# Down with seven products for five of seven pairs of weight tiles in blocks 2 and 3, and sums of GLU tiles made by adding stores to DRAM

## The chip, the core and the metric

The kernel runs on one core of one Trainium2 chip. The metric is device time in microseconds (us); the time of a kernel is the median of its runs. One execution is recorded by the hardware profiler, and its page and its trace are what this text reads. Times inside the execution count from the start of its span.

## What is computed

The input is x of shape 4 x 512 x 512, that is 2048 tokens of 512 features. The result is x plus two branches that both start from the layer-normalised tokens xn: a long convolution (S4), and a gated feed-forward network (GLU) whose three weight matrices are given as 4-bit codes with one scale for 64 values.

```python
xn = layernorm(x)                                # over the last axis
K  = s4_kernel(Lambda, p, q, B, Ct, step, 512)   # 512 taps
y  = causal_conv(xn, K) + D * xn                 # along the last axis
g  = xn @ dequant(gate_q).T                      # M = 1792 hidden features
u  = xn @ dequant(up_q).T
h  = silu(g) * u
out = x + y + h @ dequant(down_q).T
```

All of it has to come out with fp32 accuracy.

## The kernel before

**Accuracy.** TensorE multiplies in fp32r. Each operand that needs it is split into three parts, called high, low and e, and a product is three matmuls. The helper `split` makes the parts: ScalarE copies with a scale (L179), VectorE subtracts (L181), VectorE combines (L183). `split_scaled` and the Down variant at L1206 to L1210 do the same for weights.

**Tiles.** The hidden features are cut into 14 tiles of 128 rows, named m = 0 to 13; two neighbours form a pair p = m // 2, so there are seven pairs. The tokens are cut into four blocks of 512, named tb = 0 to 3. One hidden tile (m, tb) is 128 partitions x 512 numbers, 256 KB.

**Stages.** The head (layer norm, transposes, the convolution's taps, m = 0 and 1) is written out by hand, then come m = 2 to 4 and the convolution (`conv`: matmuls of 512, 384 and 256 columns at L662, of 128 at L667, evictions at L672). In m = 5 to 8 the token blocks 0 and 1 are done by Strassen's seven products in place of eight (`products_pair`), blocks 2 and 3 the standard way; in m = 9 to 13 both pairs of blocks take seven products (`products_both`, L626). Then comes Down, whose products are made block by block.

**Order.** From m = 5 on, steps are put on a list with a due time by `at(time, what, ...)`. The list is sorted, and the instructions of ScalarE, VectorE, TensorE and GpSimd are each chained in that order. SyncE's queue works in the order of the program too. An instruction that waits holds up all that stands behind it on its engine.

**Hidden tiles.** `silu` (L542, ScalarE) writes a tile h, `gated` multiplies it by the up product (L546, VectorE), and `store_hidden` (L549 and L550) stores it to the DRAM tile hd of its block and pair by SyncE, 56 stores of 256 KB. With seven products a tile u is also used: `copy_p5` (L974, ScalarE) keeps the fifth product in it, `add_up0` (L977) and `add_up1` (L981) add it, and `gated1` (L994) turns it into a finished tile, which is stored from there. The tiles live in five slots h0 to h4, which are used again and again: u in slots 0 and 1 by the pair of blocks, h in slots 2, 3 and 4. A slot is free again when its store has landed.

**Down weights.** The Down codes are loaded, turned into weights by a chain of bends (L314 on ScalarE, L324 on VectorE) and a multiplication, and stored to the DRAM tiles wdd, one for each pair, 512 KB (`down_weights` in the stretch of m = 2 to 4, `scale_down` for the last two pairs).

**Down.** For block tb and pair p, `down_product` makes 4 token tiles j x 2 weight tiles k x 3 parts = 24 matmuls of 128 x 512 (L697); 28 such steps are 672 matmuls. `load_hidden` (SyncE) brings the raw tile pair from hd into the tile stage, `hidden_part` splits it into hp; `load_split` (GpSimd, L1197) and `split_down` do the same with the weights during block 0, after which all seven pairs of weight parts stay in wdt. `load_rest` (GpSimd, L704) brings x plus the convolution from the DRAM tile rd into the tile late (1 MB a block), and `finish` (L709, VectorE) adds the bank and sends the result out.

The due times of block 0 and of what follows are set like this (STEP is 24 matmuls, D0 the start of Down):

```python
for i in range(NTB * NPR):
    tb, p = divmod(i, NPR)
    o = STEP * i
    when.setdefault(i, (
        [o + t for t in ((-8.1, -5.6, -4.45) if tb == 0 else (-11.0, -9.2, -7.8))],
        [o + t for t in (-9.2, -8.0, -6.8)],
    ))
```

Of the kernel before, what the change touches and what calls it, by code (L numbers as in the profile page):

```python
# [16 lines left out]
P = 128  # L17
# [80 lines left out]
def layernorm_s4_nf4_glu_kernel(  # L98
# [63 lines left out]
    h_dram = [[tc.dram_tile([P, 2, 512], F32, name=f"hd{b}_{p}") for p in range(NPR)] for b in range(NTB)]  # L162
    wd_dram = [tc.dram_tile([P, 2, 512], F32, name=f"wdd{p}") for p in range(NPR)]
# [21 lines left out]

    def split_scaled(dst, src):
        S.activation(dst[0], src, AF.Copy, scale=TRIM / LAM)
        V.scalar_tensor_tensor(dst[1], f(dst[0]), -LAM, src, ALU.mult, ALU.add)
        V.scalar_tensor_tensor(dst[2], src, 1.0 / OUT, f(dst[0]), ALU.mult, ALU.subtract)
# [125 lines left out]

    def parts_tile(n):
        return place([P, 3, 2, 512], F32R, f"wp_{n}")

    def decode(pair):
        if pair not in qs:  # L320
            load_weights(pair)
        q, sc, n = qs.pop(pair)
        bends(q, range(len(BENDS)))
        V.tensor_tensor(q, q, sc, ALU.mult)  # L324
        return q, n
# [219 lines left out]
    def gated(m, tb, pu, h, unit):  # L545
        V.scalar_tensor_tensor(h, pu, unit, h, ALU.mult, ALU.mult)  # L546
        store_hidden(m, tb, h)

    def store_hidden(m, tb, h):  # L549
        nc.sync.dma_start(h_dram[tb][m // 2][:, m % 2, :], h)  # L550
# [13 lines left out]
    def sums_of_tokens():  # L564
# [24 lines left out]
        whole_of(t2, x12)  # L589
        V.tensor_tensor(t2, t2, t0, ALU.subtract)  # L590
        split_scaled(s4, t2)
# [90 lines left out]

    def load_hidden(tb, p):
        nc.sync.dma_start(stage[0][:, 2 * ((tb * NPR + p) % 3), :, :], h_dram[tb][p])

    def hidden_part(tb, p, k):
        if k == 0:
            hp[tb, p] = place([P, 3, 2, 512], F32R, f"hp{tb}_{p}", (tb * NPR + p) % 4)
        split([hp[tb, p][:, i, :, :] for i in range(3)], stage[0][:, 2 * ((tb * NPR + p) % 3), :, :], (k,))

    def banks_down(tb):
        return [K[i] for i in ((6, 7, 0, 3), (1, 2, 4, 5))[tb % 2]]

    def down_product(tb, p, j):
        for k in range(2):
            for part in range(3):
                T.matmul(  # L697
                    banks_down(tb)[j], hp[tb, p][:, part, k, bass.ts(j, P)], wd(p, part, k),
                    start=(p == 0 and k == 0 and part == 0),
                    stop=(p == NPR - 1 and k == 1 and part == 2),  # L700
                )

    def load_rest(tb):
        nc.gpsimd.dma_start(late["x"][:, 0:4, :], res_dram[tb])  # L704

    def finish(tb, j):
        for i, cs in enumerate(HALVES if j == 3 and tb == NTB - 1 else (ALL,)):
            o = late["x"][:, j, cs]
# [6 lines left out]
    def down_weights(p):  # L715
        nc.sync.dma_start(wd_dram[p], decode(dd(p))[0])
# [419 lines left out]
    at(begin(5) + 1.4, open_area, "turn", 3)  # L1136
# [18 lines left out]
    def load_down_scales(p, k=None):  # L1155
# [3 lines left out]
        late["x"] = phase[0].tile([P, 6, 512], F32, tag="xs4", name="late", bufs=1)  # L1159
        q, _, n = qs[dd(p)]  # L1160
        qs[dd(p)] = (q, late["x"][:, 4:6, :], n)
# [30 lines left out]

    def open_down():
        stage.append(phase[0].tile([P, 6, 2, 512], F32, tag="xs12", name="stage", bufs=1))

    def load_split(p):
        nc.gpsimd.dma_start(stage[0][:, 2 * (p % 3) + 1, :, :], wd_dram[p])  # L1197

    def split_down(p, k):
        for i in range(len(wdt), (6 * p + 9) // 4):  # L1200
            wdt.append(work.tile([P, 4, 512], F32R, tag="xp", name=f"wdt{i}", bufs=12))
        at = [6 * p + 2 * i for i in range(3)]
        d = [wdt[s // 4][:, s % 4 : s % 4 + 2, :] for s in at]
        src = stage[0][:, 2 * (p % 3) + 1, :, :]
        if k == 0:
            S.activation(d[0], src, AF.Copy, scale=TRIM / LAM)  # L1206
        elif k == 1:
            V.scalar_tensor_tensor(d[1], f(d[0]), -LAM, src, ALU.mult, ALU.add)
        else:
            V.scalar_tensor_tensor(d[2], src, 1.0 / OUT, f(d[0]), ALU.mult, ALU.subtract)  # L1210
# [9 lines left out]
    for i in range(NTB * NPR):  # L1220
        tb, p = divmod(i, NPR)
        o = STEP * i
        when.setdefault(i, (
            [o + t for t in ((-8.1, -5.6, -4.45) if tb == 0 else (-11.0, -9.2, -7.8))],
            [o + t for t in (-9.2, -8.0, -6.8)],
        ))
        for k in range(3):
            at(D0 + when[i][0][k], hidden_part, tb, p, k)
            if tb == 0:
                at(D0 + when[i][1][k], split_down, p, k)  # L1230
        at(D0 + (-12.19 + 0.04 * i if i < 3 else when[i - 3][0][2] + 0.1), load_hidden, tb, p)
        if tb == 0:
            at(D0 + (-12.19 + 0.04 * p if p < 3 else max(when[p - 3][1][2] + 0.1, 12.1 if p == 6 else 0.0)), load_split, p)
        for j in range(4):
            at(D0 + o + 6 * MM * j, down_product, tb, p, j)
            if p == NPR - 1:
                at(D0 + o + 6 * MM * (j + 1) + 0.3, finish, tb, j)
    for tb in range(1, NTB):
        at(D0 + STEP * NPR * tb + 8.0, load_rest, tb)
# [91 lines left out]
```

## Time and profile before

| | us |
|---|---|
| median of 3 runs | 495.94 (495.21 to 496.44) |
| profiled execution, own time | 495.62 |
| its span | 493.7 |
| m = 9 begins (first product, TensorE) | 242.1 |
| m = 10 begins | 261.2 |
| Down begins | 337.2 |
| last matmul ends | 490.0 |
| TensorE busy | 488.4 |
| VectorE busy | 361.7 |
| ScalarE busy | 298.2 |
| GpSimd busy | 18.6 |

| DMA issues | engine | count | KB each | median us from issue to landing |
|---|---|---|---|---|
| hd<-h | SyncE | 42 | 256 | 2.0 |
| hd<-u | SyncE | 14 | 256 | 2.0 |
| stage<-hd | SyncE | 28 | 512 | 4.3 |
| stage<-wdd | GpSimd | 7 | 512 | 7.2 |
| late<-rd | GpSimd | 4 | 1024 | 9.2 |

Over the span the DMA engines move 81.65 MB, 165 GB/s on the mean. The clock granted to TensorE is full in all 40 slices of the page.

How to read the lines: PE is TensorE's matmuls, PEld its weight loads (which overlap), DVE is VectorE, ACT ScalarE, POOL GpSimd, SP SyncE. A group line gives line, engine, operation, out<-in, how often, then busy time and mean ns of one, then the idle time of the engine ahead of the group and what ended it. A timeline line gives start, length, engine, line, operation, and in brackets the idle time ahead. A matmul's length is longer than the distance to the next one's start, as matmuls overlap.

### The profile page before, as it was taken

Reading aid. Unit: us, or ns where it says so; the run is one execution under the profiler, and the core shown is the slowest. Engines: PE = TensorE matmul, PEld = TensorE weight load, DVE = VectorE, ACT = ScalarE, POOL = GpSimd, SP = SyncE. Lnnn points to the kernel's source line nnn. Section 1 sums busy time; section 2 is a strip of 40 time slices with the busy share of each in tenths; the row PEclk is TensorE's granted clock in tenths of the full one; section 3 lists DMA queues with packets and bytes.
Section 4 is the critical chain, followed back from the end, with each engine's and each line's share of the span. In section 5 each row is a group of like instructions: output and inputs, shape, how many; then the busy total and the mean of one; then the engine's idle time right before and its main releaser. Section 6 shows DMA issues by size and latency. Waiting matters only on the chain.

```text
span 493.7 us, 6400 instructions
## 1 busy us (share of the span) xinstructions
PE 488.4 (99%) x2257; PEld 409.4 (83%) x2257; DVE 361.7 (73%) x576; ACT 298.2 (60%) x417; POOL 18.6 (4%) x35
## 2 busy tenths in 40 slices
PE   8999999999999999999999999999999999999996
PEld 8888888888988888888888888888888888888885
DVE  5999788969459779988896776859989527437412
ACT  7998869994856787684858967849632111211200
POOL 2302000000000000000000000010000000000000
PEclk9999999999999999999999999999999999999999
DMA  8943274957895133233223323369847525624302
GB/s 291 324 147 122 63 227 152 283 182 273 271 308 171 39 112 108 73 119 129 86 86 141 114 86 136 112 237 375 308 135 260 206 86 175 209 85 162 137 0 85
DMA packets 35983, 81.65 MB, mean 165 GB/s; under 512 B 4592, under 2 KB 5104, under 8 KB 34928
## 3 DMA queue, kind: packets, MB, share of 16 engines
q1 hardware_dynamic: 34080, 73.00, 43.2%
q0 software_dynamic: 1584, 7.87, 4.5%
q10 hardware_dynamic: 288, 0.39, 0.2%
q8 instruction: 17, 0.28, 0.2%
q14 instruction: 14, 0.11, 0.1%
HBM read 54.50 MB, written 26.74 MB: 165 GB/s over the span
## 4 chain that ended last, share of the span: by engine, by line
PE 99%; POOL 0%; issue 0%; DVE 0%; DVEq 0%; POOLq 0%
PE bank L697 31%; PE bank L626 27%; PE gu L522 17%; PE bank L635 9%; PE pc L662 5%; PE bank L522 3%; PE gu L530 3%; PE warm L744 2%; PE pt L240 1%; PE pc L667 1%; PE pm L494 0%; PE pss L405 0%; PE pm L489 0%; DVE late L709 0%; DVEq L1327 0%
## 5 line engine op out<-in xcount | busy, mean ns | idle before, releaser
L697 PE MATMUL bank<-wdt,hp 128*128 128x512 f32 x672 | 152.8, 389 | 0.0
L697 PEld LDWEIGHTS bank<-wdt,hp 128*128 128x128 f32 x672 | 126.0, 188 | 26.7 <-DVE hp L183 0.4
L179 ACT ACTIVATE hp<-stage 128x1024 fp32r<-128x1024 f32 x28 | 29.4, 1056 | 81.7 <-PE bank L697 65.4
L181 DVE TENSOR_TENSOR hp<-stage,hp 128x1024 fp32r<-128x1024 f32 x28 | 34.2, 1221 | 29.3 <-ACT hp L179 29.2
L709 DVE SCALAR_TENSOR_TENSOR late<-bank,late 128x512 f32<-128x512 f32 (+1 forms) x17 | 10.8, 657 | 33.3 <-PE bank L697 33.3
L542 ACT ACTIVATE h<-bank 128x512 f32<-128x512 f32 x39 | 22.9, 591 | 20.1 <-PE bank L626 15.4
L183 DVE SCALAR_TENSOR_TENSOR hp<-hp 128x1024 fp32r<-128x1024 f32 x28 | 34.3, 1224 | 0.9
L522 PE MATMUL gu<-xhT,wp_gu 128*128 128x512 f32 x112 | 29.8, 394 | 0.0
L522 PE MATMUL gu<-xlT,wp_gu 128*128 128x512 f32 x112 | 29.1, 389 | 0.0
L522 PE MATMUL gu<-xeT,wp_gu 128*128 128x512 f32 x112 | 28.8, 389 | 0.0
L626 PE MATMUL bank<-xlT,turn 128*128 128x512 f32 x82 | 25.3, 389 | 0.0
L626 PE MATMUL bank<-xeT,turn 128*128 128x512 f32 x82 | 25.3, 389 | 0.0
L626 PE MATMUL bank<-xhT,turn 128*128 128x512 f32 x82 | 25.2, 389 | 0.0
L522 PEld LDWEIGHTS gu<-xlT,wp_gu 128*128 128x128 f32 x112 | 21.0, 188 | 4.4
L522 PEld LDWEIGHTS gu<-xeT,wp_gu 128*128 128x128 f32 x112 | 21.0, 188 | 4.4
L522 PEld LDWEIGHTS gu<-xhT,wp_gu 128*128 128x128 f32 x112 | 20.8, 188 | 4.2
L626 PE MATMUL bank<-xs,turn 128*128 128x512 f32 x90 | 22.8, 389 | 0.0
L626 PEld LDWEIGHTS bank<-xs,turn 128*128 128x128 f32 x90 | 16.9, 188 | 3.5
L546 DVE SCALAR_TENSOR_TENSOR h<-bank,h 128x512 f32<-128x512 f32 x25 | 16.8, 685 | 2.3 <-PE bank L626 1.3
L626 PE MATMUL bank<-xs_s,turn 128*128 128x512 f32 x72 | 18.3, 389 | 0.0
L626 PEld LDWEIGHTS bank<-xeT,turn 128*128 128x128 f32 x82 | 15.4, 188 | 3.2
L626 PEld LDWEIGHTS bank<-xlT,turn 128*128 128x128 f32 x82 | 15.4, 188 | 3.2
(338 smaller groups left out, 973.0 us busy)
## 6 DMA issues: line engine op xcount, KB each, us to landing
stage<-hd SPq DMA_DIRECT2D x28, 512.0 KB, 4.3
hd<-h SPq DMA_DIRECT2D x42, 256.0 KB, 2.0
xr<-in_x_dram SPq DMA_DIRECT2D x4, 1024.0 KB, 7.0
rd<-xr SPq DMA_DIRECT2D x4, 1024.0 KB, 4.9
late<-rd POOLq DMA_DIRECT2D x4, 1024.0 KB, 9.2
out_dram<-late SPq DMA_DIRECT2D x15, 256.0 KB, 2.8
hd<-u SPq DMA_DIRECT2D x14, 256.0 KB, 2.0
stage<-wdd POOLq DMA_DIRECT2D x7, 512.0 KB, 7.2
```

The source lines that it names most:

```text
L179: S.activation(dst[0], src, AF.Copy, scale=TRIM)
L181: V.tensor_tensor(dst[1], src, f(dst[0]), ALU.subtract)
L183: V.scalar_tensor_tensor(dst[2], f(dst[1]), -LAM, f(dst[0]), ALU.mult, ALU.add)
L522: T.matmul(ps, wp[:, part, k, bass.ts(c, P)], xT[tb][part][:, :, c, :], start=(part == 0 and c == 0), stop=(part == 2 and c == NC - 1),)
L530: T.matmul(ps[:, k, j.start * P : j.stop * P], w[:, k, bass.ts(c, P)], xf[tb].rearrange("p j (c q) -> p j c q", c=NC)[:, j, c, :], start=( ...
L542: S.activation(h, pg, AF.Silu, scale=unit)
L546: V.scalar_tensor_tensor(h, pu, unit, h, ALU.mult, ALU.mult)
L626: T.matmul(ps, w[:, part, bass.ts(c, P)], x[part][:, :, bass.ts(c, P)], start=(first and part == 0 and c == 0), stop=(part == 2 and c == 1 ...
L635: T.matmul(ps, blocks[c // 2][:, part, bass.ts(c % 2, P)], xT[tb][part][:, :, c, :], start=(part == 0 and c == 0), stop=(part == 2 and c = ...
L662: T.matmul(po[:, k, i * P : HD], xT[tb][part][:, jj + k, i, :], toep[:, part, 0 : HD - i * P], start=(i == 0 and part == 0), stop=False,)
L697: T.matmul(banks_down(tb)[j], hp[tb, p][:, part, k, bass.ts(j, P)], wd(p, part, k), start=(p == 0 and k == 0 and part == 0), stop=(p == NP ...
L709: V.scalar_tensor_tensor(o, banks_down(tb)[j][:, cs], OUT, o, ALU.mult, ALU.add)
```

## The change

1. **Seven products in Down.** For blocks 2 and 3 and pairs 0 to 4, the eight quarter products (two blocks, two weight tiles k, two halves of 256 output columns) become seven, p1, p5, p6, p2, p7, p3 and p4 in this order over the five pairs each, with matmuls of 256 columns (`down_blocks`). Pairs 5 and 6 of these blocks stay as they were and lie between: (2,5) behind p2, (3,5) behind p7, (2,6) behind p3, (3,6) at the end. Blocks 0 and 1 are as before. Sums of products are formed in the banks: `copy_first` and `keep_fifth` (ScalarE, 8 copies) and `add_fifth` (VectorE, 8 additions).
2. **Sums of hidden tiles.** Four of the seven products need sums of hidden tiles. They are made in new DRAM tiles sd (one for each of the five pairs, four rows of 256 KB): `store_hidden` sends each tile of blocks 2 and 3 there by GpSimd's queue, into a range of rows, the first writer of a row plainly, the later ones with `accum_op=add`. These are 23 transfers: 15 that add (one of 1 MB, eight of 768 KB, one of 512 KB, five of 256 KB) and 8 plain ones. For the signs, the tiles of block 2 of these pairs are negated in `gated`. Five stores to hd are dropped (block 3, k = 0).
3. **Sums of weights.** Four sums of quarter tiles for each pair: for pairs 0 to 2 in `down_weights`, in the tile of the scales, stored to new DRAM tiles td; for pairs 3 and 4 in Down, from the weights loaded again (`prepare_sums`). `sums_part` splits them, during block 1, into places that have come free.
4. **Places.** The tile stage is cut otherwise; the rows of `load_rest` become four tiles in the slots h0 to h3 with four loads of 256 KB a block; the places of hp change. In the stretch of m = 5, the last of the token sums (s4) and its split move from ahead of m = 5 into it, and the area "turn" is opened 6.0 us into m = 5 and not 1.4.

The core of the diff:

```diff
     def gated(m, tb, pu, h, unit):
-        V.scalar_tensor_tensor(h, pu, unit, h, ALU.mult, ALU.mult)
+        V.scalar_tensor_tensor(h, pu, unit_of(m, tb, unit), h, ALU.mult, ALU.mult)
         store_hidden(m, tb, h)
+    def unit_of(m, tb, unit):
+        return -unit if m // 2 < NSP and tb == 2 else unit
     def store_hidden(m, tb, h):
-        nc.sync.dma_start(h_dram[tb][m // 2][:, m % 2, :], h)
+        p, k = divmod(m, 2)
+        if (tb, k) != (3, 0) or p >= NSP:
+            nc.sync.dma_start(h_dram[tb][p][:, k, :], h)
+        if p < NSP and tb >= 2:
+            lo, hi = {(2, 0): (0, 3), (3, 0): (0, 4), (2, 1): (2, 3), (3, 1): (1, 4)}[tb, k]
+            new = [i for i in range(lo, hi) if (p, i) not in summed]
+            for a, b, op in (
+                (lo, hi - len(new), ALU.add), (hi - len(new), hi, ALU.bypass),
+            ):
+                if a < b:
+                    nc.gpsimd.dma_start(
+                        s_dram[p][:, a:b, :], h.unsqueeze(1).to_broadcast([P, b - a, 512]),
+                        accum_op=op,
+                    )
+            summed.update((p, i) for i in new)
...
     def down_weights(p):
-        nc.sync.dma_start(wd_dram[p], decode(dd(p))[0])
+        q, _ = decode(dd(p))
+        nc.sync.dma_start(wd_dram[p], q)
+        if p < EARLY:
+            t = scales_of[dd(p)]
+            sums_of_weights(quarters(t), q)
+            nc.sync.dma_start(t_dram[p], t)
+    def sums_of_weights(t, q):
+        (t1, t3, t4, t2), (b11, b12, b21, b22) = t, quarters(q)
+        V.tensor_tensor(t1, b11, b12, ALU.subtract)
+        V.tensor_tensor(t3, b22, b12, ALU.subtract)
+        V.scalar_tensor_tensor(t2, t1, -1.0, b22, ALU.mult, ALU.subtract)
+        V.scalar_tensor_tensor(t4, t2, -1.0, b21, ALU.mult, ALU.subtract)
...
+    def down_blocks(pair, j):
+        for n, p in pair:
+            tb, half = {"p2": (2, left), "p3": (2, right), "p5": (3, right)}.get(n, (3, left))
+            for part in range(3):
+                T.matmul(
+                    banks_down(tb)[j][:, half], blocks_in[n, p][part][:, bass.ts(j, P)],
+                    block_weights(n, p, part),
+                    start=(n == "p1" and p == 0 and part == 0), stop=False, skip_group_check=True,
+                )
+    def copy_first(j):
+        S.copy(banks_down(2)[j][:, left], banks_down(3)[j][:, left])
+    def keep_fifth(j):
+        S.copy(kept_of(j), banks_down(3)[j][:, right])
+    def add_fifth(tb, j):
+        V.tensor_tensor(
+            banks_down(tb)[j][:, right], banks_down(3)[j][:, left], kept_of(j), ALU.add
+        )
...
+    SUMS_AT = (-4.5, 2.0, 8.0, 14.5, 25.0)
+    t = D1
+    for p in range(NPR):
+        if p < NSP:
+            units.append((D1 + SUMS_AT[p], None, load_sums, (p,), sums_part, (p,), None))
+        t = standard(1, p, t, 3 if p == 0 else next_place())
+    for n, what in (("p1", (copy_first,)), ("p5", (keep_fifth,)), ("p6", (add_fifth, 2)), ("p2", ())):
+        t = seven(n, t)
+        if what:
+            after(t, *what)
+    t = standard(2, 5, t, next_place())
+    t = seven("p7", t)
+    after(t, add_fifth, 3)
+    t = standard(3, 5, t, next_place())
+    t = seven("p3", t)
+    t = standard(2, 6, t, next_place())
+    t = seven("p4", t)
+    at(t - 4.0, load_rest, 3)
+    t = standard(3, 6, t, next_place())
...
-    at(begin(5) + 1.4, open_area, "turn", 3)
+    at(begin(5) + 6.0, open_area, "turn", 3)
```

`seven(n, t)` puts the 12 matmuls of each of the five pairs on the list and registers the loads of the blocks (`load_blocks`, SyncE, 35 transfers of 256 KB from hd and sd) and their splits; `standard` does so for a step of 24 matmuls. A loop behind them gives each load and split a due time: in the order in which TensorE needs them, on VectorE 1.25 us for each part, into three rotating places.

## The prediction

> **What bounds the kernel now.** I read the page's busy shares first, then the chain that ended last, then the costliest groups.
>
> ```profile
> PE 488.4 (99%) x2257; PEld 409.4 (83%) x2257; DVE 361.7 (73%) x576; ACT 298.2 (60%) x417; POOL 18.6 (4%) x35
> PE 99%; POOL 0%; issue 0%; DVE 0%; DVEq 0%; POOLq 0%
> L697 PE MATMUL bank<-wdt,hp 128*128 128x512 f32 x672 | 152.8, 389 | 0.0
> ```
>
> TensorE works without a gap: the chain is 99% PE, and the 672 Down matmuls of L697 have no idle time before them and take 152.8 us, 227 ns each from start to start (the 389 ns are one instruction's length; they overlap). So every matmul saved counts in full, and every wait that is put before TensorE counts in full too. The table by stretches, cut at the four Down blocks, shows what room the other engines have there (columns: stretch, us, then busy time and instructions of PE, PEld, DVE, ACT, POOL, granted clock, DMA share, GB/s):
>
> ```profile
> 337.20:375.30 38.10, 38.10 (x168) 31.13 (x167) 36.11 (x35) 21.80 (x24) 2.63 (x5) 1.00 0.73 260
> 375.30:413.40 38.10, 38.10 (x170) 31.55 (x169) 20.28 (x20) 7.43 (x7) 0.53 (x1) 1.00 0.46 157
> 413.40:451.50 38.10, 38.10 (x169) 31.55 (x169) 19.31 (x19) 7.43 (x7) 0.53 (x1) 1.00 0.46 153
> 451.50:490.00 38.50, 38.50 (x170) 31.54 (x169) 15.30 (x15) 4.25 (x4) 0.53 (x1) 1.00 0.28 97
> ```
>
> VectorE is full in block 0 (36.1 of 38.1 us) and half idle in blocks 1 to 3; DMA has room from block 1 on.
>
> **TensorE's own sum.** Five of seven pairs of blocks 2 and 3 were 5 x 2 x 24 = 240 matmuls of 512 columns and become 7 x 5 x 4 x 3 = 420 of 256 columns. 512 columns cost 227 ns. For 256 columns in fp32r with a fresh weight tile each, the trace has only the convolution's runs of three:
>
> ```profile
> 127.16 0.28 PE L662 MATMUL pc<-tp,xhT 128*128 128x256 f32 x1
> 127.27 0.28 PE L662 MATMUL pc<-tp,xlT 128*128 128x256 f32 x1
> 127.39 0.28 PE L662 MATMUL pc<-tp,xeT 128*128 128x256 f32 x1
> ```
>
> Starts lie 0.11 and 0.12 us apart; over all 32 such gaps the median is 117 ns, the range 116 to 127. So -240 x 0.227 = -54.4 and +420 x 0.117 = +49.1: **-5.3 us**; at 127 ns it is -1.1.
>
> The Trainium skill, "TensorE: Matmul & The Clock Gate" (Wait — 56ns, not 53.3ns?), gives the gap of a warm clock as columns / 2.4 GHz + about 2.5 ns: 215.8 ns for 512 and 109 for 256, which would make it -51.8 + 45.8 = -6.0 and the whole sum -3.2. The rows (227 and 117) are both longer, so they decide.
>
> **VectorE in block 1.** The weight sums of all five pairs need parts, and the change puts them into the start of block 1. From 367.93, where the low part of the last block-0 tile starts before and after, VectorE has ahead of hp1_2: 9 operations of 1024 elements up to the low part of hp1_1, with 3 evictions (L709) between; rows of this stretch start 1.13 us apart (1.26 where one needs the other), and an eviction takes 0.60:
>
> ```profile
> 366.80 1.22 DVE L1210 SCALAR_TENSOR_TENSOR wdt<-stage,wdt 128x1024 fp32r<-128x1024 f32 x1
> 367.93 1.22 DVE L181 TENSOR_TENSOR hp<-stage,hp 128x1024 fp32r<-128x1024 f32 x1
> 369.19 1.23 DVE L183 SCALAR_TENSOR_TENSOR hp<-hp 128x1024 fp32r<-128x1024 f32 x1
> ```
>  So 367.93 + 9 x 1.13 + 3 x 0.60 + 0.1 = 380.0. This frees the place for the raw weights of pair 3, which land after about 0.3 + 4.3 (the median of stage<-hd, 512 KB) = 384.5; the operations left before are done by 384.1. Then four sums of 256 elements (1.5), hp1_2's low part (1.26) and its third part (1.2) end at 388.5. TensorE comes to the third part at 375.3 + 2 x 5.45 + 0.45 = 386.65. Wait: **+1.8 us**; 0 if VectorE gets ahead by an idle gap, 3 if that load takes the longer landings of this stretch. In blocks 2 and 3 the added work (8 copies of ScalarE, 8 additions and the splits of VectorE) falls on half idle engines, and of the copied banks only those added to after p7 are needed at once, by the standard products of pair 5. I cost it at 0; without that cover the addition after p7 costs 0.3.
>
> **The adding stores.** They go through GpSimd's queue, 23 transfers (9.2 MB adding, 5.2 MB plain), each behind the landing of the earlier store to the same sd tile. A hidden tile's slot is held until they land. The nearest place is at the start of m=10, where the ring of slots turns fastest:
>
> ```profile
> 262.63 1.75 SPq L550 DMA_DIRECT2D hd<-u  x2
> 266.76 1.06 ACT L974 COPY u<-bank 128x512 f32<-128x512 f32 x2
> 268.51 0.69 DVE L977 TENSOR_TENSOR bank<-bank,u 128x512 f32<-128x512 f32 x1
> ```
>
> The second store of L550 (u9_1) is issued at 264.06 and lands at 266.06; the second copy of L974 writes that slot at 267.24. Behind the copy wait a ring part on ScalarE, its low part on VectorE, and then the addition L977, which ends 1.96 us after the copy starts; p7 needs it at 272.06. So the copy can start as late as 270.1: a 768 KB adding store may take 6.0 us from issue to landing, and from then on TensorE waits one for one. No adding transfer is in the trace. Bounds: GpSimd's one transfer with the queue to itself,
>
> ```profile
> DMA to landing us min/median/max: 3.5/3.5/3.5
> ```
>
> (512 KB; first packet 1.2 us after issue, 2.0 us of packets, 0.3 to landing) makes 1.2 + 3.0 + 0.3 = 4.5 us for 768 KB. If the destination is read as well as written, so that packets take twice as long, 7.5. The queue's rows in a busy stretch (512 KB in 7 to 10 us, 1 MB in 6.2 to 11.0) reach 11. GpSimd's own 0.53 us for a transfer, in rows whose packets are some 5 KB (1584 packets for 7.87 MB on the page), may grow by about 1 with the 2 KB rows here, which lies inside these bounds. I take 7, near the doubled one, since this stretch has little other traffic: **+1.0 us**, between 0 and 5. Elsewhere in m=5 to m=9 the slots are reused some 15 us after their store, which covers up to about 10 us a transfer; GpSimd does nothing else there.
>
> The Trainium skill, "DMA: Bandwidth & Descriptors" (Anatomy of one DMA; Rules for kernel authors), gives 2.0 us + bytes / 436e3 for a transfer of this queue, an estimate of 3.8 us, no wait and a sum of -3.5; the same page says that an accumulating DMA must wait for the semaphore of an earlier one on the same bytes, which speaks against the change, as it makes chains of these stores. No run here shows the rate of one that adds.
>
> **What goes at nothing.** The down codes q_d6d come later: SyncE's queue now has the stores of the sums of pairs 1 and 2 (waiting for VectorE) and one rd store ahead of them, about 8 us. Its consumers end their evictions at 146.06 and TensorE asks for that bank at 155.06, so 9.0 us of cover; up to +1 if it is used up. The 12 operations of weight sums (0.33 us each) before m=5 and the token sums moved into m=5 lie beside TensorE's work on engines that are 60 to 73% busy. SyncE's five fewer hidden loads of 512 KB, 35 of 256 KB and five reloads in Down meet a DMA share of 0.46 and less. The five hd stores dropped save no time on the path.
>
> **Sum.** -5.3 + 1.8 + 1.0 = **-2.5 us**. The profiled execution took 495.62 us (span 493.7 and 1.9 around it), 0.3 below the median of 495.94; from it 493.1, from the median **493.4 us**.
>
> **The rivals.** (a) *The adding stores run near the plain rate* (4.5 to 6 us): no wait at m=10; for it speaks the small share of DMA in m=9, against it the second read. -5.3 + 1.8 = -3.5, 492.4; if VectorE also keeps up, 490.6. (b) *Slower: the adding stores are slow.* One mechanism, at the slot of u9_1: its store must also wait for the 256 KB add of h9_2, issued at 260.25. With 1.5 us fixed and b us per 256 KB, it lands at 260.25 + 3.0 + 4b once b is over 2.3. At the contended rows' 11 us (b = 3.2) that is 276.1, a wait of 6.0: -5.3 + 1.8 + 6.0 = +2.5, 498.4. At b = 4.2 (14 us) it is 280.1, 10.0 of wait, 502.4, and from there stores pile up in m=6 to m=9 as well. It decides, by over 0.3%, from b of about 3.0 or 10.6 us per 768 KB. For it: reading and writing DRAM for each of 2 KB rows, on a queue whose contended rows are slow. Against it: DMA has half its time free in that stage. (c) *256 columns do not hold 117 ns over hundreds.* LDWEIGHTS is 188 ns long and only overlaps, and runs of three prove little. At 127 ns, -1.1 + 2.8 = +1.7; with the waits partly hidden, about 495 to 497.5, no change. (d) *The change does not do what it says*, TensorE's count as before: excluded by the loops, which leave 432 + 420 Down matmuls.
>
> **How the numbers follow.** A measurement of this kernel can tell about 0.3%, 1.5 us, from no change: faster is below 494.45, slower above 497.43. The forecast (short waits, 492.4 to 494.4) 0.40; (a) 0.18; (c), or a wait that eats the gain, 0.14; (b) 0.28. Faster 0.58, same 0.14, slower 0.28. The range runs from 490.2 (no wait, shorter gaps) to 502.0 (b up to 14 us a store), which leaves out slower stores still, about 0.15, and little below. The likeliest sign's own range is 490.2 to 494.4.
>
> **What would show it.** Right: 420 matmuls of 256 columns 117 ns apart; TensorE idle about 1.8 us ahead of hp1_2 and about 1 at m=10's p7; a 768 KB adding store landing in 6 to 8 us. Wrong: landings over 10 us with L974 waiting for a DMA; a gap of 127 or more; any idle time of TensorE over 1 us elsewhere, above all in m=5 or at the bank of the convolution.

## The result, and the profile after

The changed kernel takes **520.33 us**, the median of 4 runs (518.85 to 522.06), against 495.57 for the kernel before beside it: 1.050 times the time, with a 95% interval of 1.046 to 1.054. The prediction was 493.4, with a range up to 502.0: 2.5 us faster was forecast, and it is 24.8 us slower. The profiled execution took 522.06 us with a span of 520.4. Of all the runs told here, two of the sums from DRAM to DRAM (532.1 and 534.5 us) fell into a slower state of the machine and are left out of its ratio.

The page of the changed kernel: engines, granted clock, GpSimd's DMA queue (packets, MB, share of 16 engines), the chain by engine (it can be followed back to 274.95 us, so its shares add up to less than 100%), and the costliest group.

```profile
PE 495.7 (95%) x2437; PEld 419.4 (81%) x2437; DVE 401.1 (77%) x641; ACT 314.1 (60%) x443; POOL 48.5 (9%) x70
PEclk9999999989998999999999899999999889999999
q0 software_dynamic: 8416, 22.29, 19.2%
PE 28%; DMA 8%; DVE 6%; issue 3%; ACT 1%; DVEq 0%; ACTq 0%; POOLq 0%
L750 PE MATMUL bank<-wdt,hp 128*128 128x512 f32 x336 | 80.9, 401 | 6.1 <-DVE hp L185 3.6
```

TensorE has the 180 matmuls more that the change asks for, but the chain, 99% PE before, is now mixed with DMA and VectorE, and the clock dips in four places. The Down group had 0.0 us of idle time ahead of it and has 6.1. So TensorE waits. Where it does is read from the same landmarks in both traces (start times after minus before), each stretch with what held TensorE at its largest gap:

| stretch | predicted, us | measured, us | what TensorE waited for |
|---|---|---|---|
| up to the convolution's first matmul | 0 | +4.6 | VectorE, behind ScalarE, behind a late load of codes of m = 5 (9.1 us to land, 4.5 before) |
| convolution, m = 2 to 4 | 0 | +5.3 | a bank of the convolution, emptied late, since the down codes were loaded late |
| m = 5 to 8 | 0 | +1.9 | small waits, the first part of the one at 265 |
| m = 9 to 13 | +1.0 | +8.3 | copies that wait for a slot: 2.2 at 265 (for a plain store of u that took 5.3 us beside an adding one, 2.0 before), 5.9 at 290 |
| Down | -5.3 + 1.8 | +6.7 | -4.1 of matmuls, +10.8 of waits (2.0 at 390, 7.8 at 408, 1.1 at 453) |
| sum | -2.5 | +26.8 | |

**The predicted place.** GpSimd's and ScalarE's timeline around the slot of u9_1, then the chain that ended last:

```profile
274.95 0.90 POOL L580 DMA_DIRECT2D sd<-h  x1 [19.92 <-DVE h L560]
280.14 1.27 POOL L580 DMA_DIRECT2D sd<-u  x1 [4.29 <-DVE turn L187]
288.21 0.58 ACT L1049 COPY u<-bank 128x512 f32<-128x512 f32 x1 [6.44 <-DMA sd<-u]
```
```profile
280.14 7.91 DMA sd<-u
290.23 54.89 PE bank L662 x234
```

The 256 KB add of h9_2 is issued at 274.95 and lands 4.7 us later; only then may the 768 KB add of u9_1 start, at 280.14, though u9_1 was ready at 278.5. This one takes 7.91 us, the copy (L1049, the old L974) waits 6.44 us for it, and TensorE starts again at 290.23, after 4.1 us of idle time and 4.3 us later than its usual step. The gap is not the whole price. The table by windows of the trace (us, busy time and instructions of PE, PEld, DVE, ACT, POOL, granted clock, DMA share, GB/s):

```profile
285.70:290.20 4.50, 0.42 (x2) 0.00 (x0) 1.06 (x3) 1.99 (x5) 0.00 (x0) 0.99 0.38 98
290.20:293.70 3.50, 3.47 (x9) 2.74 (x10) 3.43 (x9) 1.02 (x3) 0.00 (x0) 0.53 0.61 181
293.70:297.00 3.30, 3.30 (x16) 2.72 (x15) 3.16 (x7) 3.24 (x5) 0.00 (x0) 1.00 0.15 47
```

After the gap the clock is 0.53 for 3.5 us: 9 matmuls instead of 16. So this wait cost 4.3 + 1.6 = 5.9 us. The gaps that end at 106 (2.9 us idle), 163 (3.3) and 412 (3.6) are followed by a slow clock too, the last one for twice as long; the gap of 1.7 us that ends at 392 is not. The wait at 265 is shorter:

```profile
262.54 0.59 ACT L1049 COPY u<-bank 128x512 f32<-128x512 f32 x1 [4.36 <-DMA hd<-u]
```

Here the same copy waits for a plain store of u, to hd, which landed after 5.3 us. In the kernel before that store landed 0.5 us ahead of the copy.

**Ahead of the convolution.** The first line is TensorE's gap, the second ScalarE's wait ahead of it, the third the two stores to sd (768 KB adding, 256 KB plain) that run at that time and take 10.3 and 10.6 us to land:

```profile
106.20 0.80 PE L503 MATMUL pm<-s4b,s4b 128*128 128x128 f32 x2 [2.85 <-DVE s4b L498]
102.47 2.15 ACT L325 ACTIVATE q_g5u<-q_g5u 128x1024 f32<-128x1024 int32 x2 [6.27 <-DMA sc_g5u<-in_up_s_dram]
91.18 1.93 POOL L580 DMA_DIRECT2D sd<-h  x2 [0.71 <-DVE nqi L458]
```

ScalarE starts when the up codes q_g5u have landed, at 102.45 (9.1 us after their issue, 4.5 before; the load of scales that the line names lands later, at 102.83). Behind it in the order of the engines come a silu, a VectorE product and the step of the taps that TensorE waits for. No slot is in this chain: the stores to sd cost time here by slowing a load beside them.

**The convolution.** The first line is VectorE waiting for a slot of a hidden tile, in which the tokens xn of the convolution are to be put; the second is SyncE's issue of the first load of the down codes q_d6d, which was at 119.17 before; the third says why (time waited, times, longest):

```profile
132.78 0.69 DVE L685 SCALAR_TENSOR_TENSOR xn<-xhT,xlT 128x512 f32<-128x512 f32 x1 [4.65 <-DMA sd<-h]
133.70 0.33 SPq L299 DMA_DIRECT2D q_d6d<-in_down_q_dram  x1
```
```profile
SPq L299 <- DMA wdd<-q_d2d: 5.2, 1, 5.2
```

The store wdd<-q_d2d has nothing to do with the sums. It took 9.0 us to land where it had taken 2.6, beside an adding store. So the first load of the down codes came 14.5 us later, and the second, which ScalarE needs to begin, 16.7, as a store of rd ahead of it had to wait for VectorE. ScalarE's start, in the kernel before and in the changed one, and TensorE's gap:

```profile
125.22 8.71 ACT L314 ACTIVATE q_d6d<-q_d6d 128x1024 f32<-128x1024 int32 x8 [3.50 <-issue]
142.13 8.71 ACT L325 ACTIVATE q_d6d<-q_d6d 128x1024 f32<-128x1024 int32 x8 [4.01 <-issue]
163.03 1.48 PE L536 MATMUL bank<-xhT,wp_g4u 128*128 128x512 f32 x4 [3.33 <-DVE xr L708]
```

ScalarE is 16.9 us later and TensorE itself 4.6, so the codes lost 12.3 us against it. The prediction's cover of 9.0 leaves 3.3, which is the gap.

**Down.** In the chain, one transfer stands before the largest gap; VectorE then waits at the head of the sums for pair 3:

```profile
401.07 8.48 DMA stage<-wdd
```
```profile
409.57 0.43 DVE L788 TENSOR_TENSOR kept<-stage 128x256 f32<-128x256 f32 x1 [4.45 <-DMA stage<-wdd]
```

The prediction had this load land after 4.6 us; it took 8.48, and hp1_2 is split behind it. No adding store runs then: what lands beside it are three loads of load_rest of block 1 (6.4 to 8.6 us each) and output stores.

**The matmuls.** TensorE's rows of p-products in Down: 3 matmuls each, 0.36 us apart.

```profile
459.11 0.52 PE L1397 MATMUL bank<-wdt,stage 128*128 128x256 f32 x3
459.47 0.52 PE L1397 MATMUL bank<-tw,stage 128*128 128x256 f32 x3
```

The median over 416 such gaps is 120 ns, so TensorE's own sum is -240 x 0.227 + 420 x 0.120 = -4.1 us, not -5.3.

### The profile page after: what moved, and what is told of

It reads as the page before. It is cut to its first block, busy times and chain, and to the rows that moved or that the text cites. A ratio compares the mean times of both kernels' runs of the same rounds, so it can differ in the third digit from the quotient of the medians.

```text
span 520.4 us, 7020 instructions
## 1 busy us (share of the span) xinstructions
PE 495.7 (95%) x2437; PEld 419.4 (81%) x2437; DVE 401.1 (77%) x641; ACT 314.1 (60%) x443; POOL 48.5 (9%) x70
## 3 DMA queue, kind: packets, MB, share of 16 engines
q0 software_dynamic: 8416, 22.29, 19.2%
## 5 line engine op out<-in xcount | busy, mean ns | idle before, releaser
L750 PE MATMUL bank<-wdt,hp 128*128 128x512 f32 x336 | 80.9, 401 | 6.1 <-DVE hp L185 3.6
L750 PEld LDWEIGHTS bank<-wdt,hp 128*128 128x128 f32 x336 | 64.7, 194 | 21.1 <-DVE hp L185 4.0
L580 POOL DMA_DIRECT2D sd<-h x22 | 21.7, 1052 | 205.3 <-DVE h L560 176.9
L1378 ACT ACTIVATE hb_p<-stage 128x1024 fp32r<-128x1024 f32 (+1 forms) x14 | 12.3, 877 | 30.9 <-PE bank L750 20.0
L662 PEld LDWEIGHTS bank<-xhT,turn 128*128 128x128 f32 x82 | 15.4, 194 | 11.2 <-DVE bank L1052 7.1
L183 ACT ACTIVATE hp<-stage 128x1024 fp32r<-128x1024 f32 x14 | 14.7, 1052 | 13.2 <-PE bank L750 4.4
L750 PE MATMUL bank<-wdt,stage 128*128 128x512 f32 x96 | 22.5, 390 | 0.0
L185 DVE TENSOR_TENSOR hp<-stage,hp 128x1024 fp32r<-128x1024 f32 x14 | 17.1, 1221 | 5.5 <-ACT hp L183 5.5
L750 PEld LDWEIGHTS bank<-wdt,stage 128*128 128x128 f32 x96 | 17.9, 188 | 3.6
L1380 DVE SCALAR_TENSOR_TENSOR hb_p<-stage,hb_p 128x1024 fp32r<-128x1024 f32 (+1 forms) x14 | 13.9, 992 | 8.4 <-ACT hb_p L1378 8.4
```

What stands on the lines that cost most here:

```text
L183: S.activation(dst[0], src, AF.Copy, scale=TRIM)
L185: V.tensor_tensor(dst[1], src, f(dst[0]), ALU.subtract)
L580: nc.gpsimd.dma_start(s_dram[p][:, a:b, :], h.unsqueeze(1).to_broadcast([P, b - a, 512]), accum_op=op,)
L662: T.matmul(ps, w[:, part, bass.ts(c, P)], x[part][:, :, bass.ts(c, P)], start=(first and part == 0 and c == 0), stop=(part == 2 and c == 1 ...
L750: T.matmul(banks_down(tb)[j], hp[tb, p][part][:, k, bass.ts(j, P)], wd(p, part, k), start=(first and k == 0 and part == 0), stop=(last and ...
L1378: S.activation(d[0], src, AF.Copy, scale=-TRIM)
```

## The experiments

The main theory: the adding stores cost the time, by what they make wait and by slowing each transfer beside them. Its rivals: the sums of weights made early (VectorE, stores to td in SyncE's queue) cost it; or Down's own order does, and the seven products save nothing. The kernels are told in groups by what they tell apart.

### Which part costs: stores, additions, weight sums

**No stores to sd**; the products of Down read other hidden tiles (the sums are left out), the rest is as in the changed kernel.

```diff
-        if p < NSP and tb >= 2:
+        if False:
...
-            return s_dram[p][:, SOURCE[n], :]
...
+            return h_dram[tb][p][:, k, :]
```

> The changed kernel without the 23 stores to sd; the Down steps load other tiles of the same size from hd in their place (so the sums are left out). TensorE's idle gaps in the changed kernel, with the slow clock behind them: 3.5 us at 106, 5.2 at 163, 2.2 at 265, 5.9 at 290, then in Down 2.0 at 392, 7.8 at 412 and 1.1 at 453. Theory 1 (the stores to sd hold hidden slots and crowd the other transfers): the four gaps ahead of Down go, 520 - 16.8 = about 503. Theory 2 (the sums of weights, their stores and the order of SyncE's queue make the gaps at 106 and 163; sd only those at 265 and 290): about 512.

Measured: 499.64 us, 1.009 times before (95% interval 1.006 to 1.012; so written below). Of the 25 us, 20.7 go with the 23 stores. Up to Down no landmark is over 0.5 us late; three gaps in Down stay (4.1, 4.3 and 1.1 us with the slow clock behind them), so the waits there do not come from the stores to sd.

**All stores to sd plain**, the same bytes to the same rows, the additions left out:

```diff
-                        accum_op=op,
+                        accum_op=ALU.bypass,
```

> The changed kernel with all 23 stores to sd plain, in the same order and with the same waits (so the additions are left out). If the price is that of adding (the destination is read too), a 768 KB store lands in about 5 us in place of 8.4 and the gaps at 265 and 290 shrink by about 5 us: about 514. If it is the bytes and the chain of stores, nothing over 2 us: 518 to 520.

Measured: 503.86, 1.018 (1.015 to 1.021), 10 us below the figure expected for adding, which had counted the two slots alone: the gap at 106 is gone too, and of that at 163 1.6 us are left. So the stores as such cost 4.2 us and their adding 16.5. The page's DMA lines, of the changed kernel first (KB each, median us from issue to landing), then the queue and the same line with plain stores:

```profile
sd<-h POOLq DMA_DIRECT2D x10, 768.0 KB, 8.4
hd<-h SPq DMA_DIRECT2D x37, 256.0 KB, 2.6
```
```profile
q0 software_dynamic: 6176, 22.29, 12.6%
sd<-h POOLq DMA_DIRECT2D x10, 768.0 KB, 4.5
```

The same 22.29 MB take 19.2% of 520.4 us with additions and 12.6% of 501.0 without: 36.8 us more of all 16 engines for 9.2 MB. The group of 768 KB in the page mixes seven adding stores with three plain ones. Of the eight that add (u9_1 is the eighth) the median is 8.8 us (7.9 to 14.0), of the same eight made plain 4.5 (3.8 to 9.6); of the five of 256 KB that add 4.9, made plain 3.0. The prediction's "doubled" bound of 7.5 was a little low; its plain value of 4.5 is the median. The Trainium skill, "DMA: Bandwidth & Descriptors" (Anatomy of one DMA), would make it 3.8 us by its fit, an estimate; the least disturbed of the plain stores took 3.8 and agree, the adding ones are far from it.

**No early sums of weights**, no stores to td; Down loads the weights themselves (sums left out):

```diff
-        if p < EARLY:
-            t = scales_of[dd(p)]
-            sums_of_weights(quarters(t), q)
-            nc.sync.dma_start(t_dram[p], t)
```

> The changed kernel without the early sums of weights: no 12 operations of VectorE and no 3 stores of 512 KB to td in m = 2 to 4; Down loads the plain weights in their place (so these sums are left out). Theory 2: the gaps at 106 and 163 go, about 511. Theory 1: they stay, since the stores to sd make them, 518 to 520.

Measured: 520.01, 1.051 (1.047 to 1.055), the changed kernel's time. The gap at 163 is gone, but that at 106 is 5.2 us long and another, of 3.8, stands at 177, so the sum is the same. This rival falls.

**Neither**, both edits together:

```diff
-        if p < NSP and tb >= 2:
+        if False:
...
-        if p < EARLY:
...
```

> Both left out, the stores to sd and the early sums of weights. Only the Down stage of the change is left, with its gaps (2.0 + 7.8 + 1.1 = 10.9) and its saving of about 5.3: by both theories 495.6 - 5.3 + 10.9 = about 501. If theory 1 holds, this is at most 2 us below the first run; if theory 2 holds, some 10 us below it.

Measured: 499.03, 1.006 (1.004 to 1.009), as without the stores alone.

**The kernel before with the stores added**, the 23 transfers and nothing else of the change (the rows of block 2 are added without their sign, and nobody reads them):

```diff
         nc.sync.dma_start(h_dram[tb][m // 2][:, m % 2, :], h)
+        p, k = divmod(m, 2)
+        if p < NSP and tb >= 2:
...
```

> The kernel before with the 23 stores to sd added and nothing else of the change (the sums are written and never read). If the adding stores are the cause by themselves, this costs what leaving them out gave back, some 15 to 21 us: 511 to 516, with gaps of TensorE at about 163 and at the start of m = 10. If they hurt only together with the change's other work in m = 2 to 4 (sums of weights, td), less than 8 us: under 503.

Measured: 510.33, 1.029 (1.027 to 1.032): +15.2 us in a kernel without seven products in Down, just below the expected 511 to 516. Its waits carry the two slots of the changed kernel, of the convolution's tokens and of the copy of u; here the first one makes TensorE's gap of 2.4 us at 133:

```profile
DVE xn L666 <- DMA sd<-h: 5.8, 1, 5.8
ACT u L991 <- DMA sd<-u: 5.2, 1, 5.2
```

**No stores to sd before m = 5**, the first ten transfers; pairs 0 to 2 read other tiles (their sums left out):

```diff
-        if p < NSP and tb >= 2:
+        if p < NSP and tb >= 2 and m >= 5:
```

> The changed kernel without the sd stores of m = 0 to 4 (pairs 0 to 2 load other tiles in their place, their sums left out); those of m = 5 to 9 stay. If the gaps at 106 and 163 come from these early stores: 520 - 8.7 = about 511, with the gaps at 265 and 290 as before. If they come from the rest of the change in that stretch, 518 or more.

Measured: 506.51, 1.023 (1.020 to 1.026), 4.5 us below the expected 511. Both gaps before m = 5 are gone (the start of m = 5 is 0.1 us early, not 9.9 late), and m = 9 begins as before, not 11.8 late; the waits for a slot from m = 9 on stay. Leaving out the early stores gives back 13.8 us of the 25. Some of that is in Down, where the load that took 8.48 us took at most 5.4 here, so by the traces the early stores cost about 10 to 12 us, still more than those at the predicted place. No run parts, in m = 2 to 4, the slots held from the loads slowed.

**Another slot at the predicted place**: two finished tiles, (m = 8, block 1) and (m = 9, block 3), go into the tile h and not into u, so that the copies of L1049 need not wait for their stores.

```diff
-        V.scalar_tensor_tensor(u, u, OUT, h_of[m, pair, 1], ALU.mult, ALU.mult)
+        o = h if (m, pair) in ((8, 0), (9, 1)) else u
+        V.scalar_tensor_tensor(o, u, OUT, h, ALU.mult, ALU.mult)
```

> The changed kernel with one edit: the finished tiles (8,1) and (9,3) are written to slot 4, which is next used 17 us later, and not to the u slot, which is next used 3 us later. If the gap at 290 (4.3 us and 1.6 of slow clock) is the u slot held by the adding store, as predicted, it goes, and most of the 2.2 at 265: about 513. If the adding store hurts there by crowding other transfers: 519 to 521.

Measured: 515.51, 1.038 (1.033 to 1.042): 4.8 us less, where 7 was expected. The gap at 290 fell from 5.9 to 1.3 us, that at 265 from 2.2 to about 1. The cause of this wait is shown: the slot.

### Do the seven products save anything?

All three kernels here have no stores to sd (sums left out), and move steps of Down; each keeps the moves of the one before it.

**First moves**: the weight sums later, load_rest of block 0 later, the output stores of blocks 0 to 2 by GpSimd.

```diff
-    SUMS_AT = (-4.5, 2.0, 8.0, 14.5, 25.0)
+    SUMS_AT = (2.0, 9.0, 16.0, 23.0, 30.0)
-    at(D0 + 12.0, load_rest, 0)
+    at(D0 + 22.0, load_rest, 0)
```

> The changed kernel without the stores to sd (other tiles loaded in their place, the sums left out), and with the steps in Down moved: SUMS_AT from (-4.5, 2, 8, 14.5, 25) to (2, 9, 16, 23, 30), load_rest of block 0 ten us later, and the output stores of blocks 0 to 2 on GpSimd's queue. The first run left gaps of 4.1 us at 371, 4.3 at 391 and 1.1 at 432 and took 499.6. If these gaps come from the order of VectorE's work and of the loads in Down, they go and the seven products give what 240 x 0.227 - 420 x 0.120 says: 495.3 - 4.1 = about 491.2. If they come from too much work in block 1, however it is ordered, 496 or more.

Measured: 496.33, 1.002 (1.001 to 1.003), not the 491.2 hoped for. The gaps at 371 and 391 are gone; a new one of 6.3 us stands at 428 to 438, where a hidden load takes 9.4 us beside load_rest.

**load_rest due later**:

```diff
-    for tb, time in ((1, D1 + 8.0), (2, D2 + 8.0)):
+    for tb, time in ((1, D1 + 18.0), (2, D2 + 25.0)):
```

> The run without sd stores and with moved steps in Down, and the loads of rd for blocks 1 and 2 put off by 10 and 17 us (sums left out as there). The run before left one gap, 6.3 us at 428 to 438, where a 256 KB load of a block took 9.4 us to land beside 1 MB of late<-rd. If that load is the cause: the gap goes and the seven products show their whole saving, 495.2 - 4.0 = 491.2. If the blocks' own loads are too many, the gap stays, 495 to 496.

Measured: 495.89, 1.001 (0.999 to 1.003). A miss: the loads went out when they did before. GpSimd's timeline has them at 417, though their due time is some 20 us later, and the chain has the load that lands beside them:

```profile
416.95 1.60 POOL L763 DMA_DIRECT2D late<-rd  x3
```
```profile
420.35 9.16 DMA stage<-hd
```

A due time puts a step behind others in its engine's queue. With nothing before it there, it holds nothing back.

**load_rest of blocks 1 and 2 by ScalarE**, whose queue has work before it:

```diff
-            nc.gpsimd.dma_start(rest(j), res_dram[tb][:, j, :])
+            (nc.scalar if tb in (1, 2) else nc.gpsimd).dma_start(rest(j), res_dram[tb][:, j, :])
```

> The run without sd stores, with the moved steps in Down, and now with the loads of rd for blocks 1 and 2 issued by ScalarE, whose queue keeps its place among the steps (sums left out as there). In the run before, putting the due time off moved nothing: GpSimd had nothing else in its queue and issued these loads at 417 as before, and the load of a block beside them took 9.2 us. If the crowding by that 1 MB makes the last gap (4.9 us at 427 to 435): 495.2 - 4.0 = 491.2, under 493. If the loads of the blocks are too many by themselves, 495 to 496 again.

Measured: **492.28**, 0.994 (0.992 to 0.995). ScalarE issues them at 438.75, and TensorE has no gap over 0.6 us:

```profile
PE 484.4 (99%) x2437; PEld 414.9 (85%) x2437; DVE 401.9 (82%) x641; ACT 315.8 (64%) x443; POOL 27.3 (6%) x51
PEclk9999999999999999999999999999999999999999
```

So the saving of the seven products is real, in a kernel that does not make the sums they need: -2.9 us by medians, -3.3 between the traces, against -4.1 worked out. The whole of the loss is waits, with the slow clock behind them: of the 28.1 us between the changed kernel and this one, 20.7 went with the stores to sd and 7.4 with the moves in Down.

### Can the sums be had in another way?

**Sums by transfers from DRAM to DRAM**, 15 adding ones from hd to sd and 5 plain ones within sd, due from m = 5 on, so that no hidden slot waits for them:

```diff
+    def sum_rows(p, i):
+        tb, k, lo, hi = ((3, 0, 1, 4), (2, 0, 0, 3), (3, 1, 1, 4), (2, 1, 2, 3))[i]
+        src = h_dram[tb][p][:, k, :] if i else s_dram[p][:, 0, :]
+        nc.gpsimd.dma_start(
+            s_dram[p][:, lo:hi, :], src.unsqueeze(1).to_broadcast([P, hi - lo, 512]),
+            accum_op=ALU.add if i else ALU.bypass,
+        )
```

> The changed kernel with the sums of hidden tiles made later and from DRAM to DRAM: each tile is stored once (hd by SyncE, the first one of a pair to row 0 of sd by GpSimd), and 20 transfers of GpSimd's queue, 15 of them adding as before, copy and add from there between m = 5 and m = 12, at times at which no u slot is waited for. Same bytes added. If what hurts is that adding stores hold the hidden slots and crowd the busy stretch of m = 2 to 4, the four gaps ahead of Down go: 520 - 17 to 20 = 500 to 503. If adding itself, at any time, slows the other transfers enough, over 508.

Measured: 516.9 and 523.1 us, 1.050 (1.044 to 1.055): no gain. They did not come late either. GpSimd's queue has nothing else, and issued the first that adds at 85.47 us; in the chain a load of scales beside such transfers takes 8.07 us (3.0 before):

```profile
85.47 1.30 POOL L577 DMA_DIRECT2D sd<-hd  x1 [6.05 <-DMA sd<-sd]
```
```profile
242.41 8.07 DMA sc_g9u<-in_up_s_dram
```

**The same with the first moves in Down:**

```diff
-    SUMS_AT = (-4.5, 2.0, 8.0, 14.5, 25.0)
+    SUMS_AT = (2.0, 9.0, 16.0, 23.0, 30.0)
-    at(D0 + 12.0, load_rest, 0)
+    at(D0 + 22.0, load_rest, 0)
```

> The run with the sums from DRAM to DRAM, and the moved steps in Down as well: the whole computation. If both groups of gaps are closed: 495.3 - 4.1 = 491.2, at most 2 us above, and faster than the kernel before. If the late adding transfers still crowd others, 495 or more.

Measured: 522.96, 1.058 (1.055 to 1.061), where 495 or more stood for crowding. The gaps are spread over the whole span.

**Three pairs only** (2 to 4), with pair 2 summed from DRAM to DRAM, the other slot and the moves. (Some of its additions of p-products come ahead of the last pair's, so its output lacks a part of these sums; the work is all there.)

```diff
-    NSP, EARLY = 5, 3
+    SET = (2, 3, 4)
...
+    for i, time in enumerate((1.0, 9.0, 20.9, 31.0)):
+        at(begin(5) + time, sum_rows, SET[0], i)
```

> A whole kernel drawn from the runs before: seven products for pairs 2, 3 and 4 alone; no early sums of weights; pair 2's sums by four late transfers from DRAM to DRAM in m = 5 and 6, those of pairs 3 and 4 by adding stores as in the change, with the finished tiles of (8,1) and (9,3) written to slot 4 in place of the u slot; the steps of Down moved, a fourth place for the split blocks, the later loads of rd put off. The saving is 3 x (48 x 0.227 - 84 x 0.120) = 2.4 us. If each cause of a gap found so far is met: 495.2 - 2.4 = 492.8, up to 494.3 with a wait of VectorE where the seven products begin. If adding transfers crowd the others at any time: over 496.

Measured: 503.12, 1.017 (1.013 to 1.021), on the side of crowding (over 496). A load of codes again, in the chain (8.24 us to land, 3.0 before):

```profile
186.88 8.24 DMA q_g8u<-in_up_q_dram
```

**Two pairs only** (3 and 4), the whole computation, with the stores of the change, the other slot, the moves and ScalarE's loads:

```diff
-    NSP, EARLY = 5, 3
+    SET = (3, 4)
...
-            nc.gpsimd.dma_start(rest(j), res_dram[tb][:, j, :])
+            (nc.scalar if tb in (1, 2) else nc.gpsimd).dma_start(rest(j), res_dram[tb][:, j, :])
```

> A whole kernel with the least of the adding stores: seven products for pairs 3 and 4 alone (m = 6 to 9), none of the sums made in the busy stretch of m = 2 to 4, the tiles (8,1) and (9,3) in slot 4, the steps of Down moved, loads of rd for blocks 1 and 2 by ScalarE. The saving is 2 x (48 x 0.227 - 84 x 0.120) = 1.6 us. If the adding stores are free where no slot is waited for: 493.6. If each also delays what lies beside it (the gaps of m = 5 to 9 that were left with slot 4 add up to 3.6 us): 495 to 497, no gain.

Measured: **494.66**, 0.9986 (0.9977 to 0.9996). TensorE is at 99% with one gap at 277, which costs 0.9 us. Two pairs save 2/5 of 4.1, 1.6 us, and this gap takes back more than half of it. It is the best whole version found, half a microsecond under before.

**All five pairs, paced**: the whole computation, the moves of the 492.28 kernel, row tile 3's first tile stored plainly to sd, and 15 adding transfers from DRAM to DRAM, each held back by a flag that VectorE writes and GpSimd overwrites:

```diff
+    def sum_rows(p, i):
+        V.memset(flag, 0.0)
+        nc.gpsimd.memset(flag, 1.0)
+        nc.gpsimd.dma_start(s_dram[p][:, lo:hi, :], ..., accum_op=ALU.add)
```

> The whole computation, all five pairs. Row tile 3's first tile is stored plainly to all four blocks of the sum's rows; the other three additions of each pair are adding transfers from DRAM to DRAM, fifteen of them, and each is held back by a flag that VectorE sets at a chosen time from m = 5 on, so none runs beside the convolution, and at most two in one value of m. Down has the moves of the run with ScalarE's loads (492.28 us without any adding store). Theory A (an adding transfer costs only where a load that is short of cover lands beside it, and early ones do the harm): 492.3 plus at most 1.5, so 492 to 494, faster than both kernels. Theory B (each adding transfer slows whatever lands beside it, wherever it is put): fifteen of them at about 10 us each cover some 150 us of the span; the three-pair kernel lost 10.8 us against 492.3 that way, so 498 to 505.

Measured: 506.46, 1.023 (1.021 to 1.025), above even theory B's 498 to 505. The transfers did come when they were asked to, from 173 us on. The start of m = 5 is 0.2 us late, so the convolution is free of loss. But m = 9, behind two transfers in each of four values of m, starts 6.9 us late, Down 9.4, and the last matmul ends 12.5 late. Its DMA lines:

```profile
hd<-h SPq DMA_DIRECT2D x37, 256.0 KB, 3.9
sd<-hd POOLq DMA_DIRECT2D x10, 768.0 KB, 10.0
```

and the chain:

```profile
188.49 7.31 DMA q_g8u<-in_up_q_dram
404.75 9.09 DMA stage<-wdd
```

The stores of hidden tiles take 3.9 us (2.0 before), the codes q_g8u 7.31 (3.0 before). The kernel is 13.9 us under the changed one. The moves in Down alone gave 7.4 us where no sums are made (499.64 to 492.28), so at most some 6.5 can be put down to the place of the transfers. The other 14.2 us above 492.28 stay. How much of that is their number, and how much their kind (they read DRAM as well, and land after 10.0 us, not 8.8), no run parts. The flag's writes on VectorE (0.1 us each, 15 of them) were not tried apart.

## Why the prediction was wrong, step by step

**TensorE's own sum**: mechanism right, size off. -5.3 was -4.1, since 256 columns went 120 ns apart over hundreds, not 117 as in the convolution's runs of three. Rival (c) had 127 and does not hold.

**The predicted slot**: place and mechanism right, term mis-sized. A 768 KB adding store took 7.9 us where 7 was taken. Its predecessor, which the forecast did not count, held it up: a 256 KB add landed after 4.7 us, and the next was let go 5.2 us after its issue, where there was room for 3.8. Rival (b) had this chain, but with 1.5 us fixed and the rest by size it began to bite only when 768 KB took 8.4 us. As an estimate, these two transfers give about 3.1 us fixed and 1.6 for each 256 KB, so the small one is slower than the rule made it. That is 4.3 us of wait for 1.0. The slow clock behind it, 1.6 us, was in no term.

**The step that failed** is that the adding stores were priced at this one slot and at nothing everywhere else: "Elsewhere in m=5 to m=9 the slots are reused some 15 us after their store, which covers up to about 10 us a transfer", and the heading "What goes at nothing". By m = 9, ahead of the predicted place, TensorE was 11.8 us late, and leaving out the 23 stores gave back 20.7. Two things were overlooked.

- *The other transfers.* There was no term for what an adding store does to all else that lands in its time. The median hidden store went from 2.0 to 2.6 us, that of u from 2.0 to 3.3, the up codes of m = 5 from 4.5 to 9.1, one store of weights from 2.6 to 9.0. The late q_d6d was seen, with 9.0 us of cover and 8 us of delay, and the price "up to +1 if it is used up". It lost 12.3 us against TensorE, and the 3.3 that the cover left open cost 5.3 with the slow clock. The prediction's own list of signs of being wrong had idle time "at the bank of the convolution"; that is where it came.
- *The other slots.* The sentence looked for reuse from m = 5 on. In m = 2 to 4 the convolution's tokens go into the same slots, and VectorE waits there 4.65 us; in the kernel before with the stores added, this wait makes TensorE's gap. And at m = 9 a slot of u is used again 2.5 us after its store was issued, not 15, with 0.5 us of cover.

The size was within reach. GpSimd's queue had 4.5% of the span for 7.87 MB, 2.8 us of all 16 engines a MB; 14.4 MB more, and 9.2 MB read a second time, make 66 us more by this estimate, 18% of the span in all. It measured 19.2%.

**VectorE in block 1**: the wait is there, ahead of the part named, but 7.8 us with its slow clock, not 1.8, for the load took 8.48 us, not 4.6, and 2.0 more stood before it. The prediction's "3 if that load takes the longer landings of this stretch" was the right direction with too little of it. Without the stores it still cost 4.3 + 4.1 us; moved, nothing (492.28). So this term was wrong by itself: what held the load up was load_rest and the output stores, in Down's own order.

**The rivals.** (b), slower by adding stores, had the right cause with one place and 502.4 at most; it needed 14 us a store for that. The stores that add took 8.8 us in the median and cost time at four places of TensorE, three of them not the predicted one. Its chance was 0.28, and the range ended where its single slot ended, at 502.0.

## What to carry to other kernels

Price a new background transfer twice: by who waits for it, and by every transfer that lands beside it, over the whole span. In a kernel whose TensorE is at 99%, each load has a few microseconds of cover and no more (here 9.0 for the down codes, 0.5 for a slot of u). Ask of each held buffer who writes it next anywhere in the kernel, not in the stage of the change. A due time in a list delays a transfer only if its queue has work ahead of it, so put it on an engine that is busy then, or give it something to wait for.

## What the runs showed of the hardware

Here an adding transfer cost far more than its bytes: with plain stores, 14.4 MB took (12.6% of 501.0) - (4.5% of 493.7) = 40.9 us of the 16 engines, of which the 9.2 MB would be 26; adding, these cost 36.8 more, 2.4 times as much, by this estimate. From DRAM to DRAM a 768 KB one took 10.0 us.

The length of a gap of TensorE does not tell whether the slow clock follows. One of 1.8 us was followed by it (no early stores, at 381), one of 2.9 was not (the kernel before with the stores, at 285). Where the gap falls tells it: in each of the 14 traces whose clock drops on the way, the changes of the granted clock, but for the first and the last, lie whole multiples of 3.41 us apart, 60 changes in all. Cut into such windows, each of the 28 in which TensorE stood idle for over 55% at full clock was followed by one at half clock, and none of the 37 with 20 to 51%; of four between, two were. The two gaps, in windows (the first two lines hold the end of the longer gap and what follows, the others the shorter one and what follows):

```profile
283.88:287.29 3.41, 1.83 (x8) 1.53 (x9) 2.90 (x6) 1.74 (x5) 0.00 (x0) 1.00 0.43 129
287.29:290.70 3.41, 3.41 (x17) 2.81 (x16) 3.26 (x8) 2.58 (x4) 0.00 (x0) 1.00 0.28 102
377.86:381.27 3.41, 1.56 (x6) 0.76 (x5) 3.41 (x4) 0.00 (x0) 0.00 (x0) 1.00 0.43 154
381.27:384.69 3.42, 3.42 (x10) 2.64 (x9) 3.39 (x5) 1.06 (x1) 0.00 (x0) 0.50 0.51 174
```

The longer gap was cut by a window's edge into two parts, each under half a window. The Trainium skill, "TensorE: Matmul & The Clock Gate" (What's actually happening), has a gate that watches a free-running window of about 3.4 us and halves the clock after an idle one. The window agrees, in its length and in that it does not start anew with the work; but a window idle for little more than half was enough here, and the measurement decides.
